# A graph layer: one gathered chunk of every sixth group loaded row by row through SyncE, and a new order of the end's list

## The chip, the cores and the metric

The kernel runs on one core of a Trainium2 chip. The metric is the device time of one execution in microseconds (us). The kernel before took 2024.47 us (median of 3 runs, 2023.82 to 2025.51).

The engines are TensorE (PE in the profile; its weight loads are PEld), VectorE (DVE), ScalarE (ACT), GpSimd (POOL) and SyncE (SP). SyncE computes nothing here: it issues DMAs and reads register values. A name with q behind it (SPq, POOLq) is an engine's own instruction queue.

## The reference

There are N = 12,500 nodes with D = 128 features and M = 200,000 edges, sorted by their target node `dst`. Each edge has a source node `src` and a time `ew`.

```
h      = relu(layernorm(x))                        # per node
score  = (h @ W_Q.T)[dst] . (h @ W_K.T)[src] / sqrt(128) * exp(-ew)      # per edge
keep   = the 16 best scores of every dst
alpha  = softmax of the kept scores within dst
agg    = sum over the kept edges of dst: alpha * (h[src] @ W_msg.T)
out    = x + relu(h @ W_self.T + agg)
```

Every edge needs the row h[src], 512 bytes from an unforeseeable place. That is 200,000 rows.

## The kernel before

The edges are cut into chunks of P = 128 and groups of GC = 14 chunks. This gives G = 112 groups; the last has 9 chunks. A group handles the edges of about 112 nodes. Since a node's edges can reach into the next group, a group also works on the first chunk of the group behind it, so it has up to NJ = 15 chunks.

In a preparation, h is computed for all nodes and written to a table `h_tab` in the device's memory (HBM). The edges' source numbers are turned into columns (`idx_all`, one column per chunk, one edge per partition). The first four groups (RAW) are gathered from x itself.

The gathers are GpSimd's work. One indirect DMA (L176) fetches the 128 rows of one chunk into `hs[:, j, :]`. `let_go(g, k)` (L183) orders the chunks 2k and 2k+1 of group g: VectorE copies their two columns of numbers to `ix` (L191), and GpSimd then issues the gathers.

The main loop has an iteration i for every group, and at each iteration several groups are at different stages. The order on every engine is written out by hand (`manual_schedule`): each engine works through its instructions in the order in which the program names them. The stages that matter here, for the group given in brackets:

- `load_nodes` (i+3): SyncE reads a register with the group's first node (L522) and loads the nodes' rows h_r (L529) and x_t (L532).
- `more(k)`: the gathers of group i+4 or i+5, by `let_go`.
- `q_to_edges` and `scores` (i): TensorE spreads q to the edges, and VectorE multiplies it with the gathered rows (L608). The rows come from `rows_of(g, j)`.
- `slots_by_node`, `slots_out`, `node_by_slots` (i-1): scores into a table of nodes by slots (TensorE, ScalarE).
- `best`, `sum_of_exps` (i-2): the 16 best of every node (VectorE), the softmax's sum (ScalarE).
- `kept_to_edges`, `one_over_sum`, `on_edges`, `exps` (i-2): which edges are kept, back on the edges.
- `weights` and `sums` (i-3): the weights as a matrix `alz` (VectorE) and its product with the gathered rows (TensorE, L699, again by `rows_of`), in two parts; `sums_out` (ScalarE).
- `sums_turned`, `products` (i-4): the transpose of the sums and the products with W_self and W_msg (TensorE).
- `output` (L719, VectorE) and `store` (L725, SyncE, or L728, GpSimd, for the last four groups) (i-5).

SyncE's own order within an iteration is: h_r and x_t, and then the store, which waits until VectorE has written `o`.

The tile `hs` has 8 buffers, `ix` has 7, `h_r` 3, `x_t` 10 and `o` 2. All PSUM tiles of `so` (the transposes, the products) share one bank, and so do those of `et`. The bank `a` is a single buffer.

After the loop, a list written out by hand finishes the last groups (L is the last one), with four short helpers for steps that come together:

```
        def to_rows(g):
            products(g)
            output(g)
            store(g)
```

Of the kernel before, what the change touches and what calls it, by code (L numbers as in the profile page):

```python
# [10 lines left out]
F32 = mybir.dt.float32  # L11
BF16 = mybir.dt.bfloat16
I32 = mybir.dt.int32
# [4 lines left out]
SP = mybir.EngineType.SP  # L18
PSUM = bass.MemoryType.PSUM

P = 128
# [55 lines left out]
def gnn_layer(  # L77
# [94 lines left out]
    def gather(g, j0, j1, index, table=h_tab):  # L172
        if j0 == 0:
            T[g]["hs"] = rows_pool.tile([P, GC, D], F32, name="hs", bufs=8)
        for j in range(j0, j1):
            nc.gpsimd.indirect_dma_start(  # L176
                out=T[g]["hs"][:, j, :], out_offset=None, in_=table[0:N, :],
                in_offset=bass.IndirectOffsetOnAxis(ap=index(j), axis=0))

    def gather_at_once(g, table):  # L180
        gather(g, 0, own[g], lambda j: idx_all[:, GC * g + j:GC * g + j + 1], table)

    def let_go(g, k):  # L183

        j0, j1 = 2 * k, min(2 * k + 2, own[g])
        if j0 >= j1:
            return
        if k == 0:
            T[g]["ix"] = rows_pool.tile([P, GC], I32, name="ix", bufs=7)
        ix = T[g]["ix"]  # L190
        nc.vector.tensor_copy(ix[:, j0:j1], idx_all[:, GC * g + j0:GC * g + j1])  # L191
        gather(g, j0, j1, lambda j: ix[:, j:j + 1])
# [320 lines left out]
    with tc.tile_pool(name="win", bufs=2) as win:  # L513
# [2 lines left out]
        et = bank("e", 1)  # L516

        def rows_of(g, j):
            return T[g]["hs"][:, j, :] if j < GC else T[g + 1]["hs"][:, 0, :]

        def start_of(g, row, most):
# [171 lines left out]
        def sums(g, part, at=None):  # L693
            n = chunks[g]
            if part == 0:
                T[g]["pa"] = et[:, 384:384 + P] if at is None else at
            half = n // 2
            for j in range(half) if part == 0 else range(half, n):
                nc.tensor.matmul(T[g]["pa"], lhsT=alz[g % 2][:, WW * j + PRE:WW * j + PRE + P],  # L699
                                 rhs=rows_of(g, j), start=(j == 0), stop=(j == n - 1))  # L700

        def sums_out(g):
            T[g]["agn"] = win.tile([P, D], F32, name="agn")
            nc.scalar.activation(T[g]["agn"], T[g]["pa"], AF.Copy, scale=T[g]["rden"])
# [8 lines left out]
        def products(g):  # L713
            nc.tensor.matmul(so[:, 3 * P:4 * P], lhsT=T[g]["hT"], rhs=wselfT, start=True, stop=False)
            nc.tensor.matmul(so[:, 3 * P:4 * P], lhsT=T[g]["aggT"], rhs=wmsgT, start=False, stop=True)

        def output(g):
            T[g]["o"] = win.tile([P, D], F32, name="o")
            nc.vector.scalar_tensor_tensor(T[g]["o"], so[:, 3 * P:4 * P], 0.0, T[g]["x_t"],  # L719
                                           op0=OP.max, op1=OP.add)  # L720

        def store(g):

            if g < G - TAIL:
                nc.sync.dma_start(out[ds(start_of(g, 0, N - P), P), :], T[g]["o"])  # L725
            else:
                k = g - (G - TAIL)
                nc.gpsimd.indirect_dma_start(  # L728
                    out=out[:, :], out_offset=bass.IndirectOffsetOnAxis(ap=idxo[:, k:k + 1], axis=0),
                    in_=T[g]["o"], in_offset=None, bounds_check=N - 1, oob_is_err=False)  # L730

        def at(g, stage, *args):
            if 0 <= g < G:
                stage(g, *args)


        for i in range(-3, G - 1):
            at(i + 3, load_nodes)
            if i == 8:
                nc.sync.dma_start(h_tab[N:N + P, :], zpad)  # L740
                nc.sync.dma_start(x_end[XT:XT + P, :], zpad)
                nc.sync.dma_start(x_end[0:XT, :], x[N - XT:N, :])
# [81 lines left out]
        def turned(g):  # L824
            sums_turned(g)
            sums_turned_out(g)

        def all_sums(g):
            sums(g, 0, bank("a", 1)[:, 0:P])
            sums(g, 1)  # L830
            sums_out(g)

        def to_rows(g):
            products(g)
            output(g)
            store(g)

        def all_slots(g):
            for b in range(3):
# [3 lines left out]
        def kept_on_edges(g):  # L843
            one_over_sum(g)
            on_edges(g)
            exps(g)

        q_to_edges(L, 0)
        output(L - 5)
        store(L - 5)  # L850
        weights(L - 3)
        turned(L - 4)
        all_slots(L - 1)
# [2 lines left out]
        for b in range(1, blocks):  # L856
            q_to_edges(L, b)
        node_by_slots(L - 1)
        to_rows(L - 4)
        kept_to_edges(L - 2)  # L860
        all_sums(L - 3)
        scores(L, 0)
        kept_on_edges(L - 2)
        best(L - 1)
        sum_of_exps(L - 1)
        weights(L - 2)
        kept_to_edges(L - 1)
        scores(L, 1)
        turned(L - 3)
        all_sums(L - 2)  # L870
        for b in range(2, blocks):
            scores(L, b)
        scores_in_slots(L)
        all_slots(L)
        products(L - 3)
        node_by_slots(L)
        kept_on_edges(L - 1)
        weights(L - 1)
        output(L - 3)
        store(L - 3)  # L880
        best(L)
        sum_of_exps(L)
        turned(L - 2)
        pa = bank("a", 1)[:, 0:P]
        sums(L - 1, 0, pa)
        kept_to_edges(L)
        sums(L - 1, 1)
        sums_out(L - 1)
        to_rows(L - 2)
        kept_on_edges(L)  # L890
        weights(L)
        turned(L - 1)
        all_sums(L)
        to_rows(L - 1)
        turned(L)
        to_rows(L)
    assert not later
    order.close()

# [180 lines left out]
```

## Time and profile before

| what | value |
|---|---|
| time, median of 3 runs | 2024.47 us (2023.82 to 2025.51) |
| the profiled execution's own time | 2026.79 us |
| its span, first to last instruction | 2025.0 us |
| TensorE / VectorE / ScalarE / GpSimd busy | 78% / 63% / 51% / 74% |
| mean granted TensorE clock | 0.918 of full speed |
| gathers on GpSimd (L176) | 1,563, of them 1,507 from h_tab |
| DMA queue of GpSimd / of SyncE | 19.4% / 6.6% of 16 engines |
| HBM traffic | 70 GB/s over the span |

In the profile's lines, `out<-in` names the tile written and the tiles read, and x the number of instructions. In a group's line there follow the busy time and the mean duration in ns, and after the second bar the idle time of the engine just before these instructions with what ended most of it. In a line of the order in time, the first two numbers are the start and the duration in us, and the brackets hold the idle time before it. Durations of DMA instructions on SPq are those of the issue, not of the transfer. In the lines of one source line, three durations are the minimum, the median and the maximum in ns.

### The profile page before, as it was taken

The numbers are of one execution on the slowest core, as the hardware profiler recorded it, in microseconds if no ns is written. First come the engines' busy times: TensorE is split into PE (matmuls) and PEld (weight loads), VectorE is DVE, ScalarE is ACT, GpSimd is POOL, SyncE is SP. The second block draws the span as 40 slices with busy tenths as digits, with TensorE's granted clock in tenths as the row PEclk, the third lists the DMA queues.
The fourth block names the chain that finished last, engine by engine and source line by source line (L and its number), as shares of the span: only waits on it lengthen the run. The fifth ranks groups of instructions, "written<-read, shape, count | busy, mean of one in ns | idle before, by whom it ended". The sixth has DMA issues, their size and how long they took to land. (4 is left out here: it accounts for less than half of the span.)

```text
span 2025.0 us, 42221 instructions
## 1 busy us (share of the span) xinstructions
PE 1571.0 (78%) x13800; PEld 1297.0 (64%) x13801; DVE 1274.4 (63%) x7022; ACT 1023.3 (51%) x2190; POOL 1500.8 (74%) x1580
## 2 busy tenths in 40 slices
PE   0359999878887777878887878787887877788875
PEld 0247887766666666666666666666666666666664
DVE  7567778666666656666665656666666656666654
ACT  6666666544444444544454544445444444445441
POOL 6776777777777777777777777777777777777772
PEclk9979999989898989998898988999998889998898
DMA  9422322222222222222222222222222222222220
GB/s 246 157 60 60 81 69 67 69 63 64 64 66 65 66 65 65 65 63 66 65 66 65 66 65 65 65 63 65 65 66 65 66 65 65 64 63 65 66 57 23
DMA packets 101472, 143.46 MB, mean 71 GB/s; under 512 B 31063, under 2 KB 74327, under 8 KB 100480
## 3 DMA queue, kind: packets, MB, share of 16 engines
q0 software_dynamic: 50144, 102.74, 19.4%
q1 hardware_dynamic: 51102, 37.99, 6.6%
q8 instruction: 108, 1.77, 0.4%
q14 instruction: 118, 0.97, 0.2%
HBM read 126.79 MB, written 14.40 MB: 70 GB/s over the span
## 5 line engine op out<-in xcount | busy, mean ns | idle before, releaser
L176 POOL DMA_INDIRECT hs<-h_tab,ix x1507 | 1430.8, 949 | 464.0 <-issue 291.9
L608 DVE SCALAR_TENSOR_TENSOR prod<-hs,dec_all,q 128x128 f32<-128x128 f32 x1674 | 507.9, 344 | 300.0 <-DMA hs<-h_tab,ix 259.0
L561 ACT ACTIVATE far<-a,minus 128x512 bf16<-128x512 f32 (+1 forms) x447 | 294.5, 659 | 523.5 <-PE a L559 515.7
L599 PE MATMUL q<-q,to_e 128*128 128x128 f32 x3348 | 512.9, 301 | 0.0
L599 PEld LDWEIGHTS q<-q,to_e 128*128 128x128 f32 x3348 | 483.3, 213 | 34.1 <-DVE prod L608 13.5
L699 PE MATMUL e<-hs,alz 128*128 128x128 f32 x3240 | 419.0, 282 | 0.0
L699 PEld LDWEIGHTS e<-hs,alz 128*128 128x128 f32 x3240 | 377.9, 191 | 26.9 <-issue 19.2
L584 ACT ACTIVATE aw<-a 128x400 bf16<-128x400 f32 x336 | 169.4, 504 | 313.4 <-PE a L582 313.4
L638 DVE TENSOR_SCALAR ell<-slots,e 128x40 f32<-128x40 f32 x112 | 28.1, 251 | 361.6 <-PE e L624 317.6
L707 PE MATMUL s<-ident,agn 128*128 128x128 f32 x112 | 38.5, 343 | 262.7 <-DVE kept L688 260.7
L566 ACT ACTIVATE to_e<-far 128x1920 f32<-128x1920 bf16 x112 | 201.4, 1798 | 3.5
L559 PE MATMUL a<-rel,ident 112*128 112x512 bf16 (+1 forms) x447 | 194.7, 436 | 9.0 <-ACT far L561 9.0
L707 PEld LDWEIGHTS s<-ident,agn 128*128 128x128 f32 x112 | 17.0, 152 | 278.0 <-issue 274.8
L624 PE MATMUL e<-opo,sl 128*41 128x40 f32 x3348 | 189.0, 230 | 0.0
L624 PEld LDWEIGHTS e<-opo,sl 128*41 128x41 f32 x3348 | 175.3, 144 | 12.1
L608 DVE DVE_READ_ACCUMULATOR prod<-hs,dec_all,q 128x1 f32 x1674 | 138.1, 82 | 0.1
L588 ACT ACTIVATE opo<-aw 128x1200 f32<-128x1200 bf16 x112 | 134.2, 1198 | 0.1
L582 PE MATMUL a<-minus_at,pdT 32*128 32x400 bf16 x336 | 115.1, 343 | 19.6 <-ACT pdT L575 9.7
L191 DVE COPY ix<-idx_all 128x2 int32<-128x2 int32 x754 | 129.5, 187 | 0.0
L667 PE MATMUL x<-km,to_e 128*128 128x43 bf16 x1674 | 61.1, 183 | 68.1 <-DVE km L650 67.4
L667 PEld LDWEIGHTS <-to_e 128*128 128x128 bf16 x1674 | 49.7, 97 | 99.8 <-DVE km L650 97.7
L616 DVE TENSOR_TENSOR sl<-opo,s 128x600 f32<-128x600 f32 x112 | 87.6, 782 | 4.0
(184 smaller groups left out, 1662.8 us busy)
## 6 DMA issues: line engine op xcount, KB each, us to landing
hs<-h_tab,ix POOLq DMA_INDIRECT x1507
h_r<-h_tab SPq DMA_DIRECT2D x112, 64.0 KB
x_t<-in_x_dram SPq DMA_DIRECT2D x108, 64.0 KB
out_dram<-o SPq DMA_DIRECT2D x108, 64.0 KB
xg<-in_x_dram SPq DMA_DIRECT2D x2, 1400.0 KB
h_tab<-xg SPq DMA_DIRECT2D x2, 1400.0 KB
xg<-in_x_dram SPq DMA_DIRECT2D x1, 1120.0 KB
h_tab<-xg SPq DMA_DIRECT2D x1, 1120.0 KB
```

Of the source, the lines that this page charges most:

```text
L176: nc.gpsimd.indirect_dma_start(out=T[g]["hs"][:, j, :], out_offset=None, in_=table[0:N, :], in_offset=bass.IndirectOffsetOnAxis(ap=index(j ...
L191: nc.vector.tensor_copy(ix[:, j0:j1], idx_all[:, GC * g + j0:GC * g + j1])
L559: nc.tensor.matmul(pr[:, 0:n1 - n0], lhsT=upper(ident[0:RR, g:g + 1]).to_broadcast([RR, P]), rhs=rel[:, n0:n1], start=True, stop=True)
L561: nc.scalar.activation(T[g]["far"][:, n0:n1], pr[:, 0:n1 - n0], AF.Square, bias=minus)
L566: nc.scalar.activation(T[g]["to_e"][:, 0:n], T[g]["far"][:, 0:n], AF.Relu, bias=1.0, scale=-1.0)
L582: nc.tensor.matmul(pr[:, 0:400], lhsT=T[g]["pdT"], rhs=minus_at.rearrange("k w j s -> k (w j s)")[:, n0:n1], start=True, stop=True)
L584: nc.scalar.activation(T[g]["aw"][:, n0:n1], pr[:, 0:400], AF.Square)
L588: nc.scalar.activation(T[g]["opo"].rearrange("e w j s -> e (w j s)"), T[g]["aw"], AF.Relu, bias=1.0, scale=-1.0)
L599: nc.tensor.matmul(pq[:, (j - j0) * P:(j - j0 + 1) * P], lhsT=T[g]["to_e"][:, j * P:(j + 1) * P], rhs=T[g]["q"], start=True, stop=True)
L608: nc.vector.scalar_tensor_tensor(prod, rows_of(g, j), dec_all[:, c:c + 1], T[g]["pq", b][:, (j % 4) * P:(j % 4 + 1) * P], op0=OP.mult, op1 ...
L624: nc.tensor.matmul(et[0:KM + 1, STEP * j:STEP * j + WN], lhsT=sl1[g % 2][:, j, :], rhs=T[g]["ow"][:, j, :], start=False, stop=(j == n - 1))
L699: nc.tensor.matmul(T[g]["pa"], lhsT=alz[g % 2][:, WW * j + PRE:WW * j + PRE + P], rhs=rows_of(g, j), start=(j == 0), stop=(j == n - 1))
```

## The change

Fifteen groups (20, 26, 32, ... 104) are `slowly` groups. Their last own chunk, number 13, is no longer gathered by GpSimd. SyncE loads it into a tile `late` of its own, one DMA per row.

This is spread over six iterations, those from g-7 to g-2, so that the passes of one such group begin where those of the one before end: from iteration 13 to iteration 102 every iteration has one pass. The first pass also loads the 128 source numbers into one partition (`late_i`). A pass handles 22 rows, the last one 18. For each eight rows (or what is left), one instruction loads their numbers from `late_i` into SyncE's registers; then each row is loaded from `h_tab[ds(st, 1), :]` into one partition of `late`. The pass stands behind h_r and x_t of its iteration and ahead of the store.

The readers, `scores` and `sums`, take chunk 13 of such a group from `late`.

The end's list keeps its steps and gets another order. `all_sums` and `to_rows` are taken apart, so that the parts of the sums, `sums_out`, the products and the output with its store (`written`) stand at places of their own. `begun` is the first part of the sums in bank `a`.

```diff
+    PASSES = 6
+    slowly = range(20, G - 2, PASSES)
+    AT_A_TIME = -(-P // PASSES)
+    AT_ONCE = 8
...
     def let_go(g, k):
 
-        j0, j1 = 2 * k, min(2 * k + 2, own[g])
+        j0, j1 = 2 * k, min(2 * k + 2, own[g] - (g in slowly))
...
         def rows_of(g, j):
+            if j == GC - 1 and g in slowly:
+                return T[g]["late"]
             return T[g]["hs"][:, j, :] if j < GC else T[g + 1]["hs"][:, 0, :]
...
+        def some_rows(g, part):
+            c = GC * g + GC - 1
+            if part == 0:
+                T[g]["late"] = win.tile([P, D], F32, name="late")
+                T[g]["late_i"] = win.tile([1, P], I32, name="late_i")
+                nc.sync.dma_start(T[g]["late_i"], src[c * P:(c + 1) * P].rearrange("(o p) -> o p", o=1))
+            last = min(AT_A_TIME * (part + 1), P)
+            for e in range(AT_A_TIME * part, last, AT_ONCE):
+                f = min(e + AT_ONCE, last)
+                _, numbers = nc.values_load_multi_w_load_instructions(
+                    T[g]["late_i"][0:1, e:f], engines=[SP], min_val=0, max_val=N - 1,
+                    skip_runtime_bounds_check_because="nodes' numbers")
+                for k, st in enumerate(numbers):
+                    nc.sync.dma_start(T[g]["late"][e + k:e + k + 1, :], h_tab[ds(st, 1), :])
...
             at(i + 3, load_nodes)
+            for g in slowly:
+                if g - PASSES - 1 <= i < g - 1:
+                    some_rows(g, i - g + PASSES + 1)
...
-        def all_sums(g):
+        def begun(g):
             sums(g, 0, bank("a", 1)[:, 0:P])
-            sums(g, 1)
-            sums_out(g)
-
-        def to_rows(g):
-            products(g)
-            output(g)
-            store(g)
...
+        def written(g):
+            output(g)
+            store(g)
+
         q_to_edges(L, 0)
-        output(L - 5)
-        store(L - 5)
+        written(L - 5)
...
         node_by_slots(L - 1)
-        to_rows(L - 4)
+        products(L - 4)
         kept_to_edges(L - 2)
-        all_sums(L - 3)
+        begun(L - 3)
+        sums(L - 3, 1)
         scores(L, 0)
         kept_on_edges(L - 2)
+        written(L - 4)
         best(L - 1)
         sum_of_exps(L - 1)
         weights(L - 2)
+        sums_out(L - 3)
         kept_to_edges(L - 1)
         scores(L, 1)
         turned(L - 3)
-        all_sums(L - 2)
+        begun(L - 2)
         for b in range(2, blocks):
             scores(L, b)
         scores_in_slots(L)
         all_slots(L)
-        products(L - 3)
+        sums(L - 2, 1)
         node_by_slots(L)
         kept_on_edges(L - 1)
+        sums_out(L - 2)
         weights(L - 1)
-        output(L - 3)
-        store(L - 3)
+        products(L - 3)
         best(L)
         sum_of_exps(L)
+        written(L - 3)
         turned(L - 2)
-        pa = bank("a", 1)[:, 0:P]
-        sums(L - 1, 0, pa)
+        begun(L - 1)
         kept_to_edges(L)
         sums(L - 1, 1)
+        kept_on_edges(L)
         sums_out(L - 1)
-        to_rows(L - 2)
-        kept_on_edges(L)
         weights(L)
+        products(L - 2)
+        written(L - 2)
         turned(L - 1)
-        all_sums(L)
-        to_rows(L - 1)
+        begun(L)
+        sums(L, 1)
+        sums_out(L)
+        products(L - 1)
+        written(L - 1)
         turned(L)
-        to_rows(L)
+        products(L)
+        written(L)
```

## The prediction

> **What bounds the kernel now.** I read the busy table first, then GpSimd's instructions in order of time, then the groups with their waits, then the stretches, SyncE's instructions and the end.
>
> The busy table names TensorE as the busiest engine, and that misleads:
>
> ```profile
> span 2025.0 us, 42221 instructions
> ...
> PE 1571.0 (78%) x13800; PEld 1297.0 (64%) x13801; DVE 1274.4 (63%) x7022; ACT 1023.3 (51%) x2190; POOL 1500.8 (74%) x1580
> ```
>
> GpSimd (POOL) shows 74%, but in order of time it never rests. Each gather is 0.94 to 0.95 us with 0.30 us behind it, whatever is named as the releaser:
>
> ```profile
> 1013.71 0.94 POOL L176 DMA_INDIRECT hs<-h_tab,ix  x1 [0.31 <-DMA hs<-h_tab,ix]
> 1014.96 0.95 POOL L176 DMA_INDIRECT hs<-h_tab,ix  x1 [0.30 <-issue]
> 1016.22 0.95 POOL L176 DMA_INDIRECT hs<-h_tab,ix  x1 [0.30 <-DMA hs<-h_tab,ix]
> 1017.47 0.95 POOL L176 DMA_INDIRECT hs<-h_tab,ix  x1 [0.30 <-issue]
> ```
>
> From 400 to 1,900 us the stretches count 1,200 gathers in 1,500 us: one every 1.25 us, 14 of them 17.5 us, and that is the length of an iteration there. The pitch's median is 1.252 us. The groups show who pays:
>
> ```profile
> L608 DVE SCALAR_TENSOR_TENSOR prod<-hs,dec_all,q 128x128 f32<-128x128 f32 x1674 | 507.9, 344 | 300.0 <-DMA hs<-h_tab,ix 259.0
> ```
>
> VectorE sits 259 us waiting for gathered rows, at the heel of GpSimd. The orders for gathers (the ix copies) run four to five groups ahead, so GpSimd always has work. Without that bound the other engines go faster. Before about 365 us GpSimd is still ahead by the groups gathered in the preparation, and an iteration takes 13.3 us; after that 17.5. Both can be read from SyncE's stores (L725):
>
> ```profile
> 285.69 0.36 SPq L725 DMA_DIRECT2D out_dram<-o  x1
> 286.60 0.33 SPq L529 DMA_DIRECT2D h_r<-h_tab  x1
> 287.13 0.33 SPq L532 DMA_DIRECT2D x_t<-in_x_dram  x1
> 299.02 0.36 SPq L725 DMA_DIRECT2D out_dram<-o  x1
> ...
> 1015.23 0.36 SPq L725 DMA_DIRECT2D out_dram<-o  x1
> 1016.14 0.33 SPq L529 DMA_DIRECT2D h_r<-h_tab  x1
> 1016.67 0.33 SPq L532 DMA_DIRECT2D x_t<-in_x_dram  x1
> 1032.80 0.35 SPq L725 DMA_DIRECT2D out_dram<-o  x1
> ```
>
> SyncE does some 2 us of work per iteration and then stands before the store until its o is written.
>
> **The change part by part.** The sum is made against the profiled execution: 2026.8 us, of which 2025.0 span and 1.8 around it. It lies 2.3 above the median of 2024.47, and I subtract from the median.
>
> *Gathers removed.* The groups 20, 26, ... 104 are 15, and each loses one gather: 15 x 1.252 = 18.8 us off the engine that sets the pace. It is continuously busy from about 165 us on, so each one shortens its train. An iteration with 13 gathers is 16.3 us of GpSimd; the others have shown 13.3 us at full TensorE clock, 14.5 at the mean granted clock of 0.918 if all of it stretched, so they still follow. Late next is the following gather, as before. The index copy takes one column instead of two, the same VectorE instruction.
>
> *Row loads on SyncE.* A row is one register operation (37 ns), one register move (29 ns) and one DMA issue. From h_r's issue to x_t's is 0.53 us, 0.33 of it the issue, so 0.20 is everything else. The nearest issues for one partition are L284 and L286 in the preparation:
>
> ```profile
> 0.77 0.94 SPq L282 DMA_DIRECT2D src_r<-in_src_dram  x2
> 1.76 0.22 SPq L284 DMA_DIRECT2D src_r<-in_src_dram  x1
> 2.02 0.25 SPq L286 DMA_DIRECT2D src_r<-in_src_dram  x1
> ...
> L522 SPq TENSOR_LOAD <-row_i x224: 262/270/1486, 65.3 to 1979.7; - x112
> ```
>
> A row is then 0.43 us (high end, the issue as for 128 rows: 0.53), and 22 are 9.5 us (11.7). The trace has register loads of one number only, 0.27 us and some 0.05 of gap. Three loads a pass cost 1.0 us if eight numbers cost what one costs, 7.0 us if each costs its own (22 x 0.32). I take the low end, since it is one instruction, and keep 7.0 for the range. A pass is 10.4 us, and 18.7 at most. The first pass of a group also loads the numbers (0.25) and waits until they land; h_r, issued at 1016.14, had its last landing event at 1017.83, so 1.7 us: 12.4 us. Queued behind it are the store, whose next-but-one o needs the buffer, and the next h_r and x_t.
>
> What hides it: from x_t's issue (ending 1017.00) to the next store (1032.80) SyncE has 15.8 us, 15.5 at the new mean iteration of 17.53 - 1.25/6 = 17.3 us, and 15.2 without the store's own register load. 10.4 and 12.4 fit: cost nothing. If a pass took longer, the excess comes 90 times (15 groups x 6 passes); that is a rival below. In the first passes (from iteration 13) the iterations are still 13.3 us with 11.5 free, and the one first pass is late by 1 us, against some 20 us that h_r and the stores may be late (h_r is loaded a whole iteration before its use, o has two buffers).
>
> *Do rows wait for rows?* In the preparation the ninth DMA of SyncE waits for the first's semaphore: eight in flight. Eight rows take 3.4 us to issue, a landing 1.7, so no wait. The Trainium skill, "DMA: Bandwidth & Descriptors", section "Rules for kernel authors", speaks against the change: many small transfers should be coalesced, below 64 KB one pays mostly overhead. If the overhead of a row were paid one after another (the 1.7 us landing of this trace), a pass would be 37 us and the kernel some 2,000 us slower; L284 and L286, 0.26 us apart into one tile, say that it overlaps.
>
> On the register loads "Runtime: NRT & Kernel Launch", section "Instruction fetch mechanics", gives some 200 ns per register, even in bulk. By that figure, an estimate of mine, 22 numbers cost 4.4 us and a pass 13.9, which still fits; no row here shows it.
>
> *What the rows do to GpSimd.* The trace has no one-row DMA beside a gather. Between 400 and 1,900 us the gathers with no SyncE issue within them (1,025) have a mean pitch of 1.2508 us, the 172 with one or two 1.2649. All of the difference is in five gathers of 1.51 to 1.86 us, each beside a store, h_r and x_t. 2.4 us over 258 issues is 9.3 ns each. The change adds 15 x 129 = 1,935 issues: 18 us if it goes by issues, 0.1 us if it goes by bytes (512 B against 64 KB). Below nothing I see no way. A row is nearer to no traffic than to a burst of three 64 KB transfers; I take 1 us and keep 18.
>
> *Waits at the readers.* The row's DMAs end on eight semaphores, so VectorE's first read of late, and TensorE's, may need a few more wait instructions (17 to 28 ns each on SyncE's queue), 15 times. VectorE's 259 us of waiting cover that.
>
> *The end's list.* After the last gather (1986.3) the chain alternates between VectorE and TensorE:
>
> ```profile
> 1997.74 0.33 PE L707 MATMUL s<-ident,agn 128*128 128x128 f32 x1 [0.87 <-DVE o L719]
> ...
> 1999.69 0.40 PE L667 MATMUL x<-km,to_e 128*128 128x43 bf16 x9
> ...
> 2005.46 2.27 PE L699 MATMUL a<-hs,alz 128*128 128x128 f32 x18 [2.21 <-DVE alz L689]
> ...
> 2002.51 0.29 DVE L719 SCALAR_TENSOR_TENSOR o<-s,x_t 128x128 f32<-128x128 f32 x1 [2.88 <-ACT agn L704]
> 2002.72 0.14 DVE L660 TENSOR_SCALAR rden<-den 128x1 f32<-128x1 f32 x1
> ```
>
> Group L's kept edges are on TensorE from 1999.69, but VectorE starts on them only at 2002.72, since output(L-2) stands before them. I replayed the new order with the durations of this stretch. best(L) moves ahead of output(L-3), and exps(L-1) ahead of the long sums: best(L) starts at 1996.4 instead of 1997.6. TensorE's turned(L-2) waits for output(L-3) (the 0.87 above shows that it does), now at 1998.7, so the kept edges of L come later, 2000.7 to 2001.0. kept_on_edges(L) follows at once at 2001.1, its weights end at 2003.5 instead of 2005.4. The next stop is turned(L-1) behind output(L-2) at 2004.0; sums(L) starts at 2004.25 instead of 2005.46. Output(L-1) and the last two stores on GpSimd come 1.1 us earlier, the last still behind the landing of the one before. I take -1.1; -2.0 if all of the weights' gain held, +1.0 if turned(L-2) stood wholly against it.
>
> Sum: 2024.5 - 18.8 - 1.1 + 1.0 + 0 (SyncE hidden) = 2005.6.
>
> **The rivals.**
>
> *SyncE becomes the bound* (the other side). Place: the pass between x_t and the store, iterations 13 to 102. SyncE's own work is 2.3 us, so it sets the pace when a pass exceeds 15.0 us; at 15.2 (a row of 0.65 us with cheap loads) all gain is gone, and past it each us costs 90. With rows at 0.43 and each number 0.32 us: 9.5 + 7.0 + 2.3 = 18.8 us, (18.8 - 17.53) x 90 = 114 us, less 1.1: 2137. At both high ends 21.0 us: 2336. For it: no load of several numbers in the trace. Against: 4.8 us of room at the nearest rows.
>
> *Issues that stall.* x_t's issue took 0.5 to 1.57 us instead of 0.33 in five iterations in a row, every 28 (353 to 420, 842 to 912, 1332 to 1402 us). Were each row's issue to stall so (1.23), a pass is 32.5 us, and each of these three stretches costs 5 x 17.5 less the 20 of slack, 67 us: 2024.5 + 201 - 20 = 2206. Against: h_r and the store beside it are never slow, so it isn't the queue as a whole.
>
> *GpSimd is disturbed by each issue.* 18 us: 2024.5 - 18.8 - 1.1 + 18.1 = 2022.7, no change to be measured.
>
> *The rows go one after another* (the change does not do what it says, 37 us a pass plus 3.3): (40 - 17.5) x 90 = 2,025 us more, some 4050. L284 beside L286 speaks against it.
>
> **How the numbers follow.** Forecast 0.72 (its own range 2002 to 2012: the end from -2 to +1, the disturbance up to some 6, 0.6 for the runs' spread), disturbed GpSimd 0.09, SyncE the bound 0.13, stalls 0.04, one after another 0.02. About 0.2% (4 us) is what a measurement can tell from no change. Faster by more: the forecast and a fifth of the disturbed case, 0.74; same 0.07; slower 0.19. The range runs from 2002 through the disturbed case to 2028, which leaves 2 in 10 out, nearly all above.
>
> **What would show it.** The gathers at 1,492 and their pitch at 1.252 us (a mean of 1.265 there is the disturbed case); the SyncE issues for late 0.2 to 0.3 us long and 0.43 apart, a pass of 10 to 13 us, then SyncE waiting for VectorE before the store (no wait there is the SyncE case, with VectorE's or TensorE's wait on h_r or x_t in the groups); VectorE's wait for gathered rows still near 250 us; from the last gather to the last store 1.1 us less than 25.5 us. The prediction is wrong if eight numbers cost far more than one, or if a row's issue exceeds 0.65 us.

## The result, and the profile after

The changed kernel took 2007.22 us (median of 6 runs, 2003.78 to 2007.70) against 2024.83 us of the kernel before (6 runs, 2023.82 to 2025.51). The ratio is 0.9909, with an interval of 0.9899 to 0.9919: 17.6 us less. The forecast was 2005.6.

The profiled execution of the changed kernel was the fastest of its six (2003.78, a span of 2002.0), the one of before lay above its own six (2026.79, a span of 2025.0). So the two traces are 23.0 us apart where the medians are 17.6.

The page of the changed kernel, its busy table, two groups and a line of the DMA issues:

```profile
span 2002.0 us, 48362 instructions
...
PE 1564.2 (78%) x13800; PEld 1292.3 (65%) x13801; DVE 1274.2 (64%) x7022; ACT 1023.2 (51%) x2190; POOL 1486.6 (74%) x1565
...
L176 POOL DMA_INDIRECT hs<-h_tab,ix x1492 | 1418.5, 951 | 457.4 <-issue 302.6
L617 DVE SCALAR_TENSOR_TENSOR prod<-hs,dec_all,q 128x128 f32<-128x128 f32 x1659 | 503.9, 344 | 289.4 <-DMA hs<-h_tab,ix 248.4
...
late<-h_tab SPq DMA_DIRECT2D x1920, 0.5 KB
```

The gathers from h_tab are 1,492, and with the 56 from x 1,548 instead of 1,563. VectorE waits 248.4 us for gathered rows, as it did before (259.0). GpSimd still sets the pace, and its train is shorter. The last gather ends at 1967.00 instead of 1986.29, which is 19.3 us earlier. The starts of the gathers in the two traces take this apart:

| part | us |
|---|---|
| 15 gathers fewer, at 1.251 | -18.8 |
| pitch of an undisturbed gather 1.2486 instead of 1.2511 us, 1,434 times | -3.6 |
| gathers with more than 1.3 us to the next start: 27 with 9.1 us too much, before 12 with 4.6 | +4.5 |
| the train begins earlier (166.4 instead of 167.9) | -1.5 |
| sum | -19.4 |

From the last gather to the end of the span 35.0 us remain instead of 38.75. That is another 3.7 us: 2.1 up to the last store and 1.6 behind it. Nearly all of the 1.6 is in two closing instructions of GpSimd (INC_SWDGE_SEM and DRAIN), and their time follows the number of gathers in every trace of this case:

| gathers left out | kernels | the two together, us |
|---|---|---|
| 0 | before, before_again, end_only, end_alone, rows_besides | 8.70 |
| 15 | changed, after_again, rows_only, no_rows, one_number | 7.17 |
| 18 | every5, every5_b | 6.86 |
| 23 | every4, every4_b | 6.36 |

So a gather less saves some 0.1 us here too, whatever the end's list.

SyncE's instructions in order of time, for two iterations that follow each other:

```profile
988.84 0.38 SPq L734 DMA_DIRECT2D out_dram<-o  x1
989.79 0.36 SPq L538 DMA_DIRECT2D h_r<-h_tab  x1
990.35 0.36 SPq L541 DMA_DIRECT2D x_t<-in_x_dram  x1
992.62 12.56 SPq L754 DMA_DIRECT2D late<-h_tab  x22
1006.29 0.38 SPq L734 DMA_DIRECT2D out_dram<-o  x1
1007.25 0.36 SPq L538 DMA_DIRECT2D h_r<-h_tab  x1
1007.80 0.33 SPq L541 DMA_DIRECT2D x_t<-in_x_dram  x1
1008.93 11.15 SPq L754 DMA_DIRECT2D late<-h_tab  x22
1022.99 0.38 SPq L734 DMA_DIRECT2D out_dram<-o  x1
```

A pass is 11 to 13 us of row issues, and the first row comes 2.3 us behind x_t in one iteration and 1.1 in the next. The durations on line 750, which loads the numbers, and on line 754, which loads the rows (minimum, median and maximum in ns):

```profile
L750 SPq TENSOR_LOAD <-late_i x270: 531/988/2107, 274.6 to 1799.0; - x135
...
L754 SPq FUSED_REGOPS  x1920: 37/37/42, 275.4 to 1800.2; - x192
L754 SPq MOVE late<-h_tab x1920: 29/29/29, 275.4 to 1800.3; - x192
L754 SPq DMA_DIRECT2D late<-h_tab x1920: 224/228/300, 275.5 to 1800.4; - x192
```

No row's issue is slow: 0.30 us is the longest of 1,920. Two rows are 0.412 us apart (median). But a load of eight numbers has a median of 0.99 us and reaches 2.1. The trace shows two kinds. Where the first number lies at a multiple of 16 bytes in its tile, the first load of a pass takes 0.54, the second 0.78 and the third 0.98 us. Where it lies 8 bytes off, they take 1.68, 1.92 and 1.52. A pass starts at number 0, 22, 44, 66, 88 or 110. So of the six, those from 22, 66 and 110 start 8 bytes off. For the full passes (22 rows) after 700 us the loads sum to 2.4 us in the one kind and 5.1 in the other, 3.5 on the mean.

What SyncE has left shows in its waits:

```profile
SPq L734 <- DVE kept L697: 305.0, 71, 15.8
...
SPq L750 <- DMA late_i<-in_src_dram: 18.9, 15, 1.5
```

Before the change SyncE stood 1535.3 us in 106 waits before the store (L725 <- DVE kept L688). Now it is 305.0 in 71, and some of these belong to iterations without a pass. From one store's issue to the moment when SyncE is ready for the next (its last register move) the full passes after 700 us took 15.3 us with aligned numbers and 17.5 without, and those of 18 rows 15.0. The mean of all 63 passes, short ones included, is 16.0 of a period of 17.35. In the 21 full passes that start 8 bytes off, SyncE has to wait for `o` in only 9, and the mean wait is below 0.2 us. SyncE is hidden, but by 1.4 us on the mean and not by 4.8. The wait for the numbers, in the first pass of a group, is 1.3 us.

Where GpSimd was still ahead, SyncE could not keep up. The stores at 270.86, 287.22, 304.71, 319.45 and 336.60 us are 14.7 to 17.5 us apart, where they were 13.3 before. But VectorE's outputs stayed 13.3 us apart up to 364 us, as before the change: SyncE fell behind and did not set the pace. A store that followed its `o` by 0.3 us before the change came 3.4, 7.5, 8.9, 12.7, 14.1 and 16.1 us behind it in the outputs 8 to 13, and 19.6 us at the worst (output 15, at 381.5 us). Then the iterations of 17.5 us gave the time back, and by 606 us the store was again 0.3 us behind. Until then nearly every pass went into the next without a wait. No wait of VectorE for a store stands in that stretch, and its wait for gathered rows from 271 to 607 us is 39.1 us, where it was 39.2. So the lag cost nothing that shows, since the two buffers of `o` and the early loads of h_r and x_t held it.

The end, VectorE in order of time:

```profile
1978.70 0.29 DVE L728 SCALAR_TENSOR_TENSOR o<-s,x_t 128x128 f32<-128x128 f32 x1
...
1981.26 0.19 DVE L682 TENSOR_REDUCE up<-x 128x9 f32<-128x27 f32 x1 [2.01 <-PE x L676]
...
1983.17 0.53 DVE L698 TENSOR_TENSOR alz<-opo,kept 128x360 f32<-128x360 f32 x1
1983.62 0.28 DVE L728 SCALAR_TENSOR_TENSOR o<-s,x_t 128x128 f32<-128x128 f32 x1
1986.90 0.29 DVE L728 SCALAR_TENSOR_TENSOR o<-s,x_t 128x128 f32<-128x128 f32 x1 [3.00 <-ACT agn L713]
1988.80 0.29 DVE L728 SCALAR_TENSOR_TENSOR o<-s,x_t 128x128 f32<-128x128 f32 x1 [1.60 <-PE s L724]
```

The first line is output(L-3). Behind it TensorE transposes (turned(L-2)) and then turns the kept edges of L, for which VectorE waits 2.01 us. The weights of L are done at 1983.7, 16.7 us after the last gather (before 19.1), and stand ahead of output(L-2), which was first before. The last store on GpSimd begins 23.46 us after the last gather; before, 25.54.

### The profile page after: what moved, and what is told of

Same layout as the page of the kernel before. It is cut to its first block, busy times and chain, and to the rows that moved or that the text cites. A ratio compares the mean times of both kernels' runs of the same rounds, so it can differ in the third digit from the quotient of the medians.

```text
span 2002.0 us, 48362 instructions
## 1 busy us (share of the span) xinstructions
PE 1564.2 (78%) x13800; PEld 1292.3 (65%) x13801; DVE 1274.2 (64%) x7022; ACT 1023.2 (51%) x2190; POOL 1486.6 (74%) x1565
## 3 DMA queue, kind: packets, MB, share of 16 engines
q0 software_dynamic: 49664, 101.75, 19.4%
## 5 line engine op out<-in xcount | busy, mean ns | idle before, releaser
L617 DVE SCALAR_TENSOR_TENSOR prod<-hs,dec_all,q 128x128 f32<-128x128 f32 x1659 | 503.9, 344 | 289.4 <-DMA hs<-h_tab,ix 248.4
L708 PEld LDWEIGHTS e<-hs,alz 128*128 128x128 f32 x3210 | 375.7, 191 | 26.9 <-issue 19.3
L647 DVE TENSOR_SCALAR ell<-slots,e 128x40 f32<-128x40 f32 x112 | 28.2, 252 | 352.9 <-PE e L633 305.8
L591 PE MATMUL a<-minus_at,pdT 32*128 32x400 bf16 x336 | 115.3, 343 | 19.1 <-ACT pdT L584 9.6
```

What stands on the lines that cost most here:

```text
L591: nc.tensor.matmul(pr[:, 0:400], lhsT=T[g]["pdT"], rhs=minus_at.rearrange("k w j s -> k (w j s)")[:, n0:n1], start=True, stop=True)
L617: nc.vector.scalar_tensor_tensor(prod, rows_of(g, j), dec_all[:, c:c + 1], T[g]["pq", b][:, (j % 4) * P:(j % 4 + 1) * P], op0=OP.mult, op1 ...
```

## The experiments

The question was which of the parts carries the gain, what the rows cost, and how near SyncE is to being the bound. The runs came in five sets, each with its own runs of the kernel before. One thing has to be known for reading them. In four of the five sets the chip granted TensorE a clock of only 0.74 to 0.76 of full speed, instead of 0.92, and the kernel before took 3089 to 3137 us. Only the second set (before: 2030.74 us, clock 0.92) is like the first measurement. So each set is read by its own comparison, and sizes from the others don't carry over to a clock of 0.92. The times in us that were expected for the first and third sets were worked out for 0.92.

### The two kernels again, and each half alone (first set, clock 0.74)

before_again is the kernel before, after_again the changed one.

> The kernel before once more, for a second profile of it on the chip of the other three runs. In the first two profiles the gathers that are not disturbed follow each other every 1.2511 us before the change and every 1.2486 us after it; over 1,548 gathers that is 3.9 us of the 23.0 us between the two spans. If the pitch belongs to the execution and not to the change, it takes either value here and the same as in the three other runs of this call. If the change itself shortens it, it is 1.2511 here and in the run with the end's list alone, and 1.2486 in the two runs with rows.

> The changed kernel once more, timed beside the others: 2,006 to 2,008 us, a ratio of 0.991. Undisturbed pitch as in the run before it, 20 to 30 gathers longer than 1.3 us after 165 us (12 in the first profile of before), which together cost 4 to 5 us more than before.

end_only has the new list at the end and no slow groups:

```diff
-    slowly = range(20, G - 2, PASSES)
+    slowly = range(0, 0)
```

> The new order of the end's list alone; no group is loaded row by row. My working of the end gave 1.1 us. The trace of the changed kernel has 23.5 us from the last gather to the last store instead of 25.5: by that, 2.1 us faster than before. The rival: everything behind the last gather belongs to the list, 38.8 to 35.0 us, so 3.7 us faster; then GpSimd's closing instructions (INC_SWDGE_SEM and DRAIN, 8.7 us before, 7.2 after) depend on it.

rows_only has the row loads and the old list:

```diff
-        def begun(g):
+        def all_sums(g):
             sums(g, 0, bank("a", 1)[:, 0:P])
+            sums(g, 1)
+            sums_out(g)
+
+        def to_rows(g):
+            products(g)
+            output(g)
+            store(g)
...
```

> The row loads alone, with the old list at the end. Fifteen gathers less are 18.8 us; the longer gathers take some 4 us back: 14.5 to 16 us faster than before. The rival, that the disturbance is nothing and the end carries the rest: 18.8 us faster.

Measured against 3137.05 us:

| kernel | us | ratio |
|---|---|---|
| before_again | 3136.16 | 1.0003 (0.9994 to 1.0012) |
| after_again | 3111.34 | 0.9917 (0.9902 to 0.9931) |
| end_only | 3135.73 | 0.9993 (0.9984 to 1.0002) |
| rows_only | 3111.77 | 0.9926 (0.9912 to 0.9940) |

The row loads carry the gain: alone they have all of it that can be told from the whole. The list alone is worth 0 to 5 us here. The ratio 0.991 that was expected for the changed kernel came, but not for the reason of the first chip. The page of before_again with the granted clock, and GpSimd's waits:

```profile
span 3134.4 us, 42221 instructions
...
PEclk9867776677777777776667777777776666777779
```

```profile
POOL hs L176 <- PE e L699: 594.9, 100, 6.1
POOL hs L176 <- DVE prod L608: 429.4, 106, 6.3
```

An iteration takes 27.3 us here, and GpSimd has 14 gathers in 17.5. It waits over 1,000 us for `hs` buffers that TensorE and VectorE have yet to read, so it is not the bound. Why taking one gather in 84 away still saves 25 us was not settled. The traces show where: the iteration in which GpSimd issues the 13 gathers of a slow group, every sixth, takes 25.6 us on the mean in after_again and 25.0 in rows_only (from output to output), where the same iterations take 27.0 in before_again and end_only. No wait names the cause.

The pitch of a gather is 1.2507 and 1.2508 us in before_again and after_again, 1.2480 in end_only and 1.2509 in rows_only. So the 1.2486 of the first trace after the change is a value that one execution or another has, and no effect of the change.

### The gathers without the rows, and the rows without the missing gathers (second set, clock 0.92)

no_rows leaves the loads of the numbers and rows out. One DMA of 64 KB puts 128 fixed rows of h_tab into `late`, so the scores and sums of chunk 13 in the slow groups are those of other rows:

```diff
         def some_rows(g, part):
...
-                nc.sync.dma_start(T[g]["late_i"], src[c * P:(c + 1) * P].rearrange("(o p) -> o p", o=1))
-            last = min(AT_A_TIME * (part + 1), P)
-            for e in range(AT_A_TIME * part, last, AT_ONCE):
...
-                    nc.sync.dma_start(T[g]["late"][e + k:e + k + 1, :], h_tab[ds(st, 1), :])
+                nc.sync.dma_start(T[g]["late"], h_tab[0:P, :])
```

> The fifteen gathers are left out and nothing replaces them row by row: late is filled with the first 128 rows of the table by one plain DMA (so chunk 13 of those groups is not its own rows). This is the gain without the price. If the 1,935 issues of the change lengthen gathers (3.6 us more in gathers above 1.3 us between 400 and 1,850 us, 4.5 us after 165 us, in the first two profiles), it is 18.8 for the gathers and about 2 for the end, 20 to 22 us faster than before and some 4 us faster than the changed kernel; gathers above 1.3 us as few as before (5 between 400 and 1,850 us). If those longer gathers are chance, it is as fast as the changed kernel, 17 to 18 us.

rows_besides does the opposite: every row is loaded by SyncE, and GpSimd gathers all chunks as well. The readers take the gathered rows.

```diff
-        j0, j1 = 2 * k, min(2 * k + 2, own[g] - (g in slowly))
+        j0, j1 = 2 * k, min(2 * k + 2, own[g])
...
-            if j == GC - 1 and g in slowly:
-                return T[g]["late"]
```

> All rows are loaded by SyncE as in the changed kernel, but the fifteen gathers stay and the readers take chunk 13 from hs. This is the price without the gain: the end's list is the new one, 2 us. If issues disturb gathers as the profile counts them, 4 us: 2 us slower than before. If each issue costs what I kept as the high end (9.3 ns), 16 us slower. If they cost nothing, 2 us faster. SyncE's pass still fits beside 14 gathers; if it did not, the store would follow the rows without a wait and the iterations would be longer than 17.5 us.

Measured against 2030.74 us: no_rows 2009.34, ratio 0.9899 (0.9884 to 0.9914); rows_besides 2026.52, ratio 0.9979 (0.9970 to 0.9988).

The row loads cost nothing that can be measured. With them the change had 0.9909, without them 0.9899; the two intervals overlap, and the difference is 2.0 us with some 3.7 us of uncertainty (the two half-widths, 0.0010 and 0.0015, added as squares). So a price of up to some 6 us isn't excluded by these two alone. With the rows and without the missing gathers the kernel is not slower but 4.2 us faster. That is the new list and whatever the rows cost, together. And SyncE's whole reserve of waiting comes back when the rows go. Its waits in no_rows:

```profile
SPq L734 <- DVE kept L697: 1511.7, 106, 16.0
```

In rows_besides, where they stay:

```profile
SPq L732 <- DVE kept L695: 322.9, 72, 15.9
```

Some 1,200 us of SyncE's time are spent on rows, and the time of the kernel doesn't answer to it.

The pair also settles where the additional long gathers come from (more than 1.3 us to the next start). From 400 to 1850 us there were 5 before the change and 19 after (5.9 us too much instead of 2.2). no_rows, which has no row issues, has 17 (5.6 us). rows_besides, which has all of them, has 6 (2.0 us). So they come with the missing gather and not with the issues. In the changed kernel 13 of the 19 sit at the fourth chunk of groups 27, 33, 39 and so on to 99, one behind each slow group and 104 us apart. One of them in GpSimd's order of time:

```profile
813.10 0.94 POOL L176 DMA_INDIRECT hs<-h_tab,ix  x1 [0.30 <-issue]
814.35 1.31 POOL L176 DMA_INDIRECT hs<-h_tab,ix  x1 [0.30 <-issue]
815.97 0.94 POOL L176 DMA_INDIRECT hs<-h_tab,ix  x1 [0.30 <-issue]
```

The instruction itself is longer, and no wait stands before it. What stands beside it is VectorE's `output`. Two instructions of the same stretch, and two from an iteration whose gather is not long:

```profile
814.35 1.31 POOL L176 DMA_INDIRECT hs<-h_tab,ix  x1 [0.30 <-issue]
...
814.83 0.28 DVE L728 SCALAR_TENSOR_TENSOR o<-s,x_t 128x128 f32<-128x128 f32 x1
...
832.17 0.28 DVE L728 SCALAR_TENSOR_TENSOR o<-s,x_t 128x128 f32<-128x128 f32 x1
832.20 0.94 POOL L176 DMA_INDIRECT hs<-h_tab,ix  x1 [0.31 <-issue]
```

Of the 27 long gathers of the changed kernel, 26 begin 0.20 to 0.64 us before an output, and in the four traces at a clock of 0.92 it is 74 of 79 (0.20 to 0.71 us). They end 0.7 to 0.83 us after the output began. From 165 us on, no gather of the usual length begins in that place in any of the four. So a gather is long when VectorE's run of short instructions there (a copy to `ix`, the output, the kept weights) falls into its middle, and leaving one gather out moves the train against VectorE's order. SyncE's store, h_r and x_t, which follow the output, are not the cause: while the stores lagged, the long gathers at 296.6, 323.2, 397.8 and 501.9 us stood beside an output with none of those issues during them. What in VectorE's instructions holds the gather no run tested.

The ends of these two kernels, with the new list, took 25.45 us from the last gather to the last store, as the old list did, where the changed kernel took 23.46. The stretches from the last gather to the last store say why. The columns are the length, the busy time of PE, PEld, DVE, ACT and POOL with their instructions, the granted clock, the share of the DMA engines and GB/s. The changed kernel:

```profile
1967.00:1990.50 23.50, 16.92 (x164) 15.25 (x162) 14.40 (x62) 4.02 (x16) 3.04 (x4) 1.00 0.05 15
```

no_rows, its second half and the whole:

```profile
1984.00:1997.30 13.30, 9.71 (x72) 8.97 (x72) 3.54 (x14) 1.89 (x8) 3.00 (x4) 0.87 0.05 15
1971.85:1997.30 25.45, 19.28 (x172) 17.56 (x170) 14.83 (x65) 4.02 (x16) 3.00 (x4) 0.93 0.04 13
```

The kernel before:

```profile
1986.30:2011.80 25.50, 17.13 (x164) 15.19 (x162) 14.81 (x66) 3.80 (x16) 3.00 (x3) 1.00 0.04 11
```

At the full clock the new list takes 2.1 us less than the old one (23.46 against 25.54, one trace each). With TensorE held back in the last 13 us (0.87 there, in rows_besides too) it is as long as the old one at full clock. What the old list takes at that clock no trace shows.

### The list alone, and SyncE's work made longer (third set, clock 0.74 to 0.76)

end_alone repeats end_only.

> The end's list alone once more, on a chip whose TensorE is not held back as it was in the first try. Two runs now bound it: with rows but all gathers 4.2 us faster than before (2.4 to 6.1), and the first trace of the changed kernel, 2.1 us less from the last gather to the last store. If the rows cost GpSimd nothing, this is 2 to 4 us faster than before, like the run with rows besides. My working of the end gave 1.1. If rows do cost 2 to 4 us, it is 6 us or more.

every5 and every4 have more slow groups with more rows in a pass (18 groups with 28 rows, 23 with 32):

```diff
-    PASSES = 6
+    PASSES = 5
...
-    AT_A_TIME = -(-P // PASSES)
+    AT_A_TIME = 28
```

```diff
-    PASSES = 6
+    PASSES = 4
```

> Every fifth group (18 of them) in five passes of 28 rows, the last of 16; each load of eight numbers then begins at a multiple of 16 bytes. From the trace of the changed kernel: a row is 0.41 us, a load of eight 0.54 to 0.98 us where it begins at a multiple of 16 bytes and 1.5 to 1.9 us where it lies 8 bytes off. SyncE's work is then 28 x 0.41 + 3.2 + 3.2 = 17.9 us in four iterations and some 11.5 in the fifth, 16.7 on the mean, with 17.3 at hand: it fits, and three gathers less are 3.7 us less than the changed kernel, 21 to 24 us faster than before. If SyncE is at its limit already, single passes over 17.3 us are not made good by the others, and it is no faster than the changed kernel, or slower.

> Every fourth group (23 of them) in four passes of 32 rows, all loads at multiples of 16 bytes. SyncE's work is 32 x 0.41 + 3.2 + 3.2 = 19.5 us per iteration, and GpSimd's 16 to 17.5: SyncE sets the pace from iteration 15 to 106, the store follows the rows without a wait. 92 x 19.7 us instead of 3 x 13.3 + 89 x 17.5, less some 17 us that the last groups make good: 2,200 to 2,230 us, 9 to 10% slower than before, although eight more gathers are saved than in the changed kernel. If SyncE's lateness can be absorbed (h_r, x_t and o have buffers), it is 28 us faster than before.

one_number loads each row's number by itself:

```diff
-    AT_ONCE = 8
+    AT_ONCE = 1
```

> The changed kernel with a load of its own for each row's number. With 0.27 to 0.33 us for each, as the loads of one number in the trace of before, a pass of 22 rows is 16.5 us and SyncE's work 19.3, 16.5 in the last pass: SyncE sets the pace, 2,130 to 2,170 us. If a load behind a row's issue takes 0.54 us (as the store's own does in the changed kernel), SyncE's work is 24 us and the kernel 2,550 to 2,650 us. If the load of several numbers saved nothing, it is as fast as the changed kernel.

Measured against 3102.46 us. The changed kernel was not run in this set, so it stands below with its ratio from the first. SyncE's work is taken over the full passes after 700 us, from a store's issue to the moment when SyncE is ready for the next, other waits included:

| kernel | us | ratio | SyncE's work in a pass, of a period of | passes in which it waits for `o` |
|---|---|---|---|---|
| after_again (first set) | 3111.34 | 0.9917 (0.9902 to 0.9931) | 23.6 of 26.8 | all |
| end_alone | 3101.85 | 0.9997 (0.9986 to 1.0009) | no passes | |
| every5 | 3103.22 | 1.0004 (0.9994 to 1.0014) | 29.6 of 29.7 | 9% |
| every4 | 3109.18 | 1.0028 (1.0017 to 1.0039) | 27.4 of 27.5 | 8% |
| one_number | 3110.04 | 1.0027 (1.0014 to 1.0040) | 28.2 of 28.3 | 9% |

The 2 to 4 us expected of end_alone can't be told (its interval reaches from 4.3 us faster to 2.8 slower). The slowdown by 5% and more that was expected of every4 and one_number did not come: here SyncE's work of 27 to 28 us a pass only just fills an iteration, which takes 27.3 us without it. Where SyncE still waits for `o`, the change gains; where it no longer does, the gain is gone, and with every4 and one_number a little more than it. For these two the waits of VectorE show the way back. In every4:

```profile
DVE o L728 <- DMA out_dram<-o: 256.2, 46, 8.0
```

In one_number:

```profile
DVE o L728 <- DMA out_dram<-o: 197.1, 31, 8.8
```

VectorE cannot write `o`, since the store that reads its buffer went out late. Neither before_again nor after_again has such a wait. It is what SyncE as the bound looks like. every4's SyncE in order of time goes from one pass into the next with nothing between:

```profile
1500.00 17.18 SPq L754 DMA_DIRECT2D late<-h_tab  x24
1518.00 0.39 SPq L734 DMA_DIRECT2D out_dram<-o  x1
1518.98 0.35 SPq L538 DMA_DIRECT2D h_r<-h_tab  x1
1519.53 0.33 SPq L541 DMA_DIRECT2D x_t<-in_x_dram  x1
1519.96 0.29 SPq L746 DMA_DIRECT2D late_i<-in_src_dram  x1
1522.55 20.64 SPq L754 DMA_DIRECT2D late<-h_tab  x32
1544.01 0.39 SPq L734 DMA_DIRECT2D out_dram<-o  x1
```

every5 has another wait. Its SyncE stands in front of the first row of nearly every group until TensorE has read the `late` of two groups before, since that tile has two buffers:

```profile
SPq L754 <- PE e L708: 280.5, 16, 20.5
```

So every5 doesn't measure more rows alone: spread over its 64 full passes after 700 us, this wait is 4.4 of their 29.6 us. every4 has it once.

Two things could be read from the loads. In every5 and every4 all of them start at multiples of 16 bytes, and they take 0.5 to 0.95 us, none the 1.5 to 2.1. In one_number a load of one number behind a row's issue takes 0.494 us (median), not the 0.27 of the profile of before, and 22 of them sum to 8.8 us (8.5 on the mean of all passes, those of 18 rows included).

### More groups again (fourth and fifth set)

every4_b and every5_b are the kernels every4 and every5 without another edit. The clock was low again: the kernel before took 3104.65 and 3088.97 us in these sets.

> Every fourth group in passes of 32 rows once more, since in the first try TensorE was held back and no engine of this question set the pace. As before: SyncE's work is some 19.5 us per iteration and GpSimd's 16 to 17.5, so SyncE sets the pace from iteration 15 to 106 and the store follows the rows without a wait: 9 to 10% slower than the kernel before on this chip. If SyncE's lateness is absorbed, some 30 us (1.5%) faster than before.

> Every fifth group in passes of 28 rows once more. Where TensorE is not held back: SyncE's work 17.9 us in four iterations and 11.5 in the fifth, 16.7 on the mean with 17.3 at hand. If lateness of single passes is made good by the short one, 21 to 26 us faster than before and 3.7 us faster than the changed kernel; if not, no faster than the changed kernel. Where TensorE is held back as in three calls before (granted clock 0.75), no difference from before to be measured, as in the first try.

Measured: every4_b 3109.55 us, ratio 1.0012 (0.9995 to 1.0028); every5_b 3093.9 us, ratio 1.0015 (1.0004 to 1.0026). Both have lost the gain, as in the third set; the 9 to 10% that were expected of every4_b did not come. Whether more groups pay at a clock of 0.92, where an iteration is 17.4 us and SyncE has 1.4 left, stays open. There the same rows would have to fit into two thirds of the time.

## Why the prediction held, point by point

**What bounds the kernel.** Right. GpSimd's train of gathers set the pace before and after, and TensorE at 78% did not. The runs show it where the clock is 0.92: no_rows and the changed kernel save 21.4 and 17.6 us, and 15 gathers at the pitch are 18.8. With the gathers back and all else as in the changed kernel but for the readers (rows_besides), 4.2 us are saved. With the clock at 0.74 it is not the bound, and the agreement of 25 us with the 19 there has no reason that was shown.

**The gathers removed, -18.8.** Measured in the trace at 15 x 1.251 = 18.8. The following iterations kept up, and the next gather came late next, as said. What was overlooked is the 1.5 us that 15 gathers less save in GpSimd's closing instructions (8.70 to 7.17).

**The row loads hidden.** Right in the sign, and the room was mis-sized. A row was 0.412 us instead of 0.43. The term that failed is "three loads a pass cost 1.0 us if eight numbers cost what one costs": in full passes they took 2.4 or 5.1 us, 3.5 on the mean, by the place of the first number. With that, SyncE's work was 16.0 us instead of 12.7. Of the 3.3 us more, 2.6 are the loads (3.6 on the mean of all 63 passes); the rows took 0.7 less than the 9.5 (0.412 us each, and 18 in every sixth pass), and some 1.3 remain that I didn't take apart. The prediction kept 7.0 us for the loads as its other end, and the truth lay in the middle. Of 4.8 us of room 1.4 were left. In the first passes the prediction had one of them late by 1 us; the stores lagged by up to 19.6 us there, of the some 20 that it allowed. So the row loads were hidden with almost nothing to spare, and that they were is in part luck.

The Trainium skill, "Runtime: NRT & Kernel Launch", section "Instruction fetch mechanics", has some 200 ns per register even in bulk, and the page means register loads from HBM; the prediction turned it into 4.4 us a pass as an estimate. The 3.5 us that were measured for 22 numbers, loaded from `late_i`, are nearer to it than to the 1.0 that I took, but the page has a cost per register, and here it is the alignment that decides: eight numbers cost 0.5 to 1.0 us or 1.5 to 2.1.

**Do rows wait for rows?** They don't: 0.412 us apart, no issue above 0.30. The rule of the Trainium skill that spoke against the change, to coalesce small transfers ("DMA: Bandwidth & Descriptors", section "Rules for kernel authors"), is about what a transfer costs. Here 1,920 transfers of 512 B were paid by a queue that has 14.3 us of idle time per iteration without them (1511.7 us in 106 waits), and rows_besides, 4.2 us faster than the kernel before, shows no price of theirs for the kernel.

**What the rows do to GpSimd, +1 (0 to 18).** The size was 3.5 us too small, though far nearer than 18, and the cause was wrong. The long gathers cost 4.5 us more than before instead of 1. But they are there without the rows (no_rows) and absent with them (rows_besides), and 26 of the 27 begin just before a VectorE output. In the prediction's words, "2.4 us over 258 issues is 9.3 ns each" took five long gathers for an effect of the issues beside them, where VectorE's output stands just ahead of those issues; the rows, 1,920 issues, added none. The rival of 18 us, made from that same quotient, falls with it.

**Waits at the readers.** VectorE's wait for gathered rows went from 259.0 to 248.4, and no new wait on `late` stands among VectorE's or TensorE's. As said.

**The end's list, -1.1 (-2 to +1).** Larger than forecast: from the last gather to the last store -2.1 us in the traces, with the clock at 1.00 in both. turned(L-2) waited for output(L-3) as foreseen, and kept_on_edges(L) came at 14.3 us behind the last gather, where 14.8 was worked out (1986.3 to 2001.1). sums(L) came at 17.2 instead of 18.0. The replay was right in the order and 0.5 to 0.8 us too late in its steps. Compared in time, rows_besides gains 4.2 us (2.4 to 6.1) with that list; where its other 2 us come from I can't say, and at the clock of 0.74 the list is worth nothing that can be told.

**The sum.** 2024.5 - 18.8 - 1.1 + 1.0 = 2005.6 against 2007.2. In place of these terms, the traces give -18.8, +4.5, -2.1 and the -1.5 of the closing instructions, that is 2006.6; the faster pitch of the profiled execution isn't counted, since it is not the change's. The errors of +3.5, -1.0 and -1.5 go against each other, and that the sum came within 1.6 us is luck to that extent.

**The rivals.** SyncE as the bound did not come, but was nearer than the chance of 0.13 says: in 12 of the 21 full passes that start 8 bytes off SyncE does not wait at all. With one number per load the work would have been 16.0 - 3.6 + 8.5 = 20.9 us of a period of 17.35, which over 90 passes is some 320 us (an estimate from the 8.5 us that one_number's loads sum to on the mean of its passes; on such a chip it was not run). So by this estimate it was the load of eight that decided the sign. Issues that stall, and rows one after another, did not occur.

## What to carry to other kernels

An idle queue can take work off the engine that sets the pace, even in a wasteful form; what counts is its time from one deadline to the next, here from store to store, with every register load in it. Work out that room with the dearest row for each unknown price, and look after the change at how often the queue still waits, and how far it lags while it doesn't: a queue that no longer waits is the next bound as soon as the buffers behind it are used up. When a slowdown stands beside some instruction, take that instruction away and the suspected cause away in separate runs before a price per instruction is made of it.

## What the runs showed of the hardware

- A load of six to eight numbers from one partition into SyncE's registers takes 0.54 to 0.98 us (medians) from a multiple of 16 bytes and 1.5 to 1.9 us from 8 bytes beside it (2.1 at the most). A load of one number takes 0.27 us by itself and 0.49 right behind a DMA's issue (one_number).
- SyncE issues a one-row DMA (512 B, the address from a register) in 0.228 us, 0.412 us apart in a stream at the clock of 0.92 of TensorE, and no gather of GpSimd was longer for it (6 long ones in rows_besides, 5 before). In after_again (clock 0.74) the rows are 0.74 us apart (median), but in every4 (0.75) 0.45, so the clock alone doesn't explain it.
- A gather that begins 0.20 to 0.71 us before VectorE's `output` takes 1.03 to 1.55 us instead of 0.95 (74 of the 79 long ones in four traces, and no usual one begins there). Taking one gather out of a regular train of 84 brought another one, six iterations apart and at the same chunk, into that place.
- GpSimd's two closing instructions take some 0.1 us less for each gather left out: 8.70 us with all, 7.17 with 15 fewer, 6.36 with 23 fewer.
- The same kernel took 2025 us and, on chips that granted TensorE a clock of 0.75, 3090 to 3140 us. The durations on VectorE and GpSimd hardly changed (0.34 and 0.95 to 0.96 us for the same instructions). GpSimd, whose gathers followed each other 0.30 us apart at 0.92, then waited 1,024 us for `hs` buffers that TensorE and VectorE had yet to read.
